# Attention's turn in another order: projection a turn later, values as 128x32 products, transposes together, modulations by DVE and POOL, banks in strict turn

## The chip, the cores and the metric

The kernel runs on one core of one Trainium2 chip. The metric is the device time of one execution, in microseconds (us). The kernel before takes 1629.52 us, the median of three runs (1629.29 to 1629.86).

## What is computed

The input x holds 128 sequences of 64 tokens with 128 channels, all in float32. Beside it come a condition vector for each sequence (cond) and a context of the same shape as x (ctx). Four layers follow one another:

```python
x = L0(x, cond, ctx)   # self-attention, cross-attention to ctx, MLP; modulation and gates from silu(cond)
x = L1(x, ctx, cond)   # cross-attention, both sides modulated
x = L2(x, cond, ctx)   # like L0, with the context normalised
x = L3(x, cond, ctx)   # attention of one head, router, three experts, gate
```

The attention of L0, L1 and L2 has 16 heads of 8 channels. For each of them: `xm = norm(x) * (1 + scale) + shift`, then q, k and v as products of xm (or of the context) with weights, `softmax(q k^T / sqrt(8)) v`, a projection, and a sum onto x (gated in self-attention). The change concerns these attentions alone: five of them, called here L0s, L0c, L1c, L2s and L2c (s: self, c: cross).

## The kernel before, in words

The 8192 tokens are 16 groups of 512 (8 sequences each); x stays in SBUF as 16 tiles. The program runs, one after another: L0s and L0c as one stream of 32 attention units (a unit is one group in one attention), the MLP of L0, then L1c, L2s and L2c as one stream of 48 units, the MLP of L2, and layer 3. The order of instructions is written out by hand (a manual schedule); each engine takes its own list strictly in order, and waits on semaphores where a tile isn't ready or a buffer isn't free.

In a unit:

- `prepare` (a generator: each `yield` ends a piece) loads the context (L394), measures x on DVE (`stats`, L313) and takes the power on POOL (L329, L330), normalises x on POOL (L369, L372), transposes on PE and takes the result out of PSUM (L342, then L347/L348, L359 or L379), makes k (`pk` L436, `kT` L438 on ACT, and on POOL the four masked copies `kbd` L444), q (`pq` L449, `qT` L451), and the values (`pvv` L459 on PE, two copies into `vbd` by ACT, L464 and L465).
- `scores` is called for two halves u = 0, 1: 16 products into `sc` (L478), which fills four PSUM banks and has one buffer; DVE takes the maximum `mx` (L485) and the difference `e` (L487).
- `turned` transposes a quarter of e into `pp` (L503; two banks, one buffer) and ACT takes the exponential `eT` (L507). It is called twice for each half, gg = 0 and 1.
- `weighted` multiplies by `vbd` into `po` (L520); ACT copies it to `o` (L528). The sums of the softmax come along as extra columns.
- `finish` sends the sums through DRAM (SP's queue: `sums`, `rc`, four shifts `o<-o`), takes the reciprocal on DVE (L547), sends it out (`recs`) and back spread over partitions (`rb`, L554), with two loads of the gate table (`gt`, L278) in self-attention; POOL then multiplies `oT = o * rb` (L557) and adds the bias onto x (L559); PE projects (`py`, L563); a cross unit adds py onto x on DVE (L565), a self unit makes `y = py * gate` on DVE (L568) and adds it onto x on POOL (L569).

`attend` weaves the units. Step k = 2i + u does the scores of unit i, half u, the first `turned` of the half before, the `weighted` of the half before that, then pieces of `prepare` and `finish` of neighbouring units (`go(prep, i + d)`, `go(fin, i - d)`), then the second `turned`, and more pieces. Two steps, one unit, make a turn.

The small PSUM tiles (`pk`, `pq`, `pvv`, `psT`, `po`, `py`) share one pool with two buffers, one tag "mm".

Of the kernel before, what the change touches and what calls it, by code (L numbers as in the profile page):

```python
# [59 lines left out]
def tile_kernel(ctx: ExitStack, tc: tile.TileContext, a: dict, out: bass.AP):  # L60
# [66 lines left out]
    class Places:  # L127
# [8 lines left out]

    pools = [
        Places(),
        stack.enter_context(tc.tile_pool(name="mm", bufs=2, space=PSUM)),
        None,  # L140
        None,
        None,
# [15 lines left out]
    def psum_for_mlp():  # L158
        take_psum(("ph", 4), ("py", 2))

    def mm(name):
        return pools[1].tile([P, 512], F32, tag="mm", name=name)

# [171 lines left out]

    def transposed(psum, src):

        ps = psum.tile([P, 512], F32, tag="mm", name="psT")  # L340
        for t in range(TT):
            T.transpose(ps[:, ts(t, P)], src[:, t, :], ident)  # L342
        return ps
# [23 lines left out]
    def normed_by_pool(pool, src, mv, rs, tag, engine=G):  # L367
# [6 lines left out]
            )  # L374
        return xn

    def copied(pool, ps, tag):
        t = pool.tile([P, NT], F32, tag=tag, name=tag)
        S.copy(t, ps)  # L379
        return t  # L380
# [5 lines left out]
    def prepare(pools, at):  # L386

        pool, psum = pools[:2]
        s, layer = at["s"], at["layer"]
        eps = 1e-5 if layer == "L1c" else 1e-6  # L390
        cross = layer[2] == "c"
        if cross:
            c = pool.tile([P, TT, P], F32, tag="c", name="c", bufs=3)
            nc.sync.dma_start(c, ctx_d[s])  # L394
        yield
        if layer == "L1c":
            mv = x_mv[:, s]
            rs = inv_std(pool, mv, eps)
        else:
            mv, rs = stats_of(pool, xs[s], eps)  # L400
        yield
        xn = normed_by_pool(pool, xs[s], mv, rs, "xn", V if at.get("first") else G)
        if cross:
            cn = c
            if layer != "L0c":
                cn = pool.tile([P, TT, P], F32, tag="cn", name="cn", bufs=1)
                for t in range(TT):
                    rs, nb = (v[:, s, ctx_eps.index(eps), t : t + 1] for v in (ctx_rs, ctx_nb))

                    if layer == "L1c" or s == 0:  # L410
                        G.tensor_scalar(cn[:, t, :], c[:, t, :], rs, nb, ALU.mult, ALU.add)
                    else:
                        S.activation(cn[:, t, :], c[:, t, :], AF.Identity, bias=nb, scale=rs)
        yield
        if layer == "L1c":
            kv_in = modulated_by_batch(pool, transposed(psum, cn), "L1_xcond_Wss_kv", 0, 1, s, "cm")
        elif cross:
            kv_in = copied(pool, transposed(psum, cn), "cm")
            if layer == "L0c":
                nc.sync.dma_start(ctxT[s], kv_in)  # L420
        else:
            q_in = kv_in = modulated_by_batch(
                pool, transposed(psum, xn), at["wmod"], 1, 0, s, by_dve=at.get("first", False)
            )
        yield
        if not cross:
            pass
        elif layer == "L1c":
            q_in = modulated(pool, transposed(psum, xn), "L1_xcond_Wss_q", 0, 1, s)
        else:  # L430
            q_in = copied(pool, transposed(psum, xn), "xm")
        yield


        pk = psum.tile([P, 512], F32, tag="mm", name="pk")
        T.matmul(pk, at["wk"], kv_in, start=True, stop=True)  # L436
        kT = pool.tile([P, NT], F32, tag="kT", name="kT")
        S.activation(kT, pk, AF.Identity, bias=at["bk"])  # L438
        i = turn[0] % 2
        turn[0] += 1  # L440
        vbd = vbds[i]
        kbd = pool.tile([P, 4, NB, L], F32, tag="kbd", name="kbd")
        for j in range(4):
            (V if at.get("first") else G).tensor_scalar(  # L444
                kbd[:, j], by_batch(kT), mask[:, j : j + 1], 1.0, ALU.mult, ALU.mult
            )
        yield
        pq = psum.tile([P, 512], F32, tag="mm", name="pq")
        T.matmul(pq, at["wq"], q_in, start=True, stop=True)  # L449
        qT = pool.tile([P, NT], F32, tag="qT", name="qT")  # L450
        S.activation(qT, pq, AF.Identity, bias=at["bq"])  # L451
        at.update(qT=qT, kbd=kbd)
        yield

        wv_pair = at["wv"].rearrange("p (i j d) -> p j i d", j=2, d=HD)
        pvv = psum.tile([P, NB, L], F32, tag="mm", name="pvv")
        for b in range(NB):
            for j in range(2):
                T.matmul(  # L459
                    pvv[ts(j, L), b, :], kv_in[:, ts(b, L)], wv_pair[:, j],  # L460
                    start=True, stop=True,
                )
        pv4 = pvv.rearrange("p b (i d) -> p b i d", d=HD)
        S.copy(vbd[0:L, :, :, 0:HD], pv4[0:L])  # L464
        S.copy(vbd[L:P, :, :, HD : 2 * HD], pv4[L:P])  # L465
        at["vbd"] = vbd
# [42 lines left out]
    def weighted(pools, at, u, eT):  # L509


        pool, psum = pools[:2]
        po = psum.tile([P, 2, 256], F32, tag="mm", name="po")
        e7 = eT.rearrange("p a h (g i t q) -> p a h g i t q", g=2, i=2, t=2)

        for i in range(2):
            for t2 in range(2):
                for h in range(2):
                    for g in range(4):
                        T.matmul(  # L520
                            po[ts(g, 32), i, ts(2 * t2 + h, L)],
                            at["vbd"][:, 4 * u + 2 * t2 + h, 2 * g + i, :],
                            e7[:, g // 2, h, g % 2, i, t2, :],
                            start=True, stop=True,
                        )
        if u == 0:
            at["o"] = pool.tile([P, 2, NT], F32, tag="o", name="o", bufs=3)
        S.copy(at["o"][:, :, ts(u, 256)], po)  # L528

    def finish(pools, at):  # L530
# [19 lines left out]

        if not cross:
            gt = gate_tile(pool, s, at["wp"])
        rb = pool.tile([P, NT], F32, tag="rb", name="rb", bufs=1)
        nc.sync.dma_start(rb, recs.unsqueeze(1).broadcast_to([16, HD, NT]))  # L554
        yield
        oT = pool.tile([P, NT], F32, tag="oT", name="oT", bufs=1)
        G.tensor_tensor(oT, o[:, 0, :], rb, ALU.mult)  # L557
        bias = proj_bias[at["wp"]].unsqueeze(1).broadcast_to([P, TT, P]) if cross else gt[:, :, 1, :]
        G.tensor_tensor(xs[s], xs[s], bias, ALU.add)  # L559
        yield  # L560
        py = psum.tile([P, TT, P], F32, tag="mm", name="py")
        for t in range(TT):
            T.matmul(py[:, t, :], oT[:, ts(t, P)], w[at["wp"]][:, 0], start=True, stop=True)  # L563
        if cross:
# [6 lines left out]
    def attend(pools, ats):  # L571
# [5 lines left out]
        def go(gens, i):  # L577
            if 0 <= i < n:
                next(gens[i], None)
# [8 lines left out]
        def step(k, between=(), late=()):  # L588
            i, u = divmod(k, 2)
            now, last, past = (  # L590
                halves[k - d] if 0 <= k - d < 2 * n else None for d in range(3)
            )
            if now:
                now["e"] = scores(pools, now["at"], now["u"])
            for f in between:
                f()
            if last:
                last["eT"] = pools[0].tile([P, 2, 2, 512], F32, tag="eT", name="eT")
                turned(pools, last["e"], last["eT"], 0)
            if past:  # L600
                weighted(pools, past["at"], past["u"], past["eT"])
            if u == 0:
                go(fin, i - 2)
                go(prep, i + 4)
                go(prep, i + 1)
                go(fin, i - 3)
            else:
                go(prep, i + 1)
            if last:
                turned(pools, last["e"], last["eT"], 1)  # L610
            if u == 0:
                go(prep, i + 2)
                go(prep, i + 3)
            else:
                go(prep, i + 1)
                go(prep, i + 2)
                for f in late:
                    f()
                go(fin, i - 1)
                go(fin, i - 2)  # L620
                go(prep, i + 4)

        return ahead, [lambda *more, k=k: step(k, *more) for k in range(2 * n + 5)]

    def attention_of(s, layer):
        if layer[2] == "s":
# [49 lines left out]
    def mlp(wmod, w1, b1, w2, b2, beside, mv_out=None, by_token=False):  # L676
# [50 lines left out]
            )  # L727

        def leave(d):
            pt = psum.tile([P, 512], F32, tag="mm", name="psB")  # L730
            for t in range(TT):
                T.transpose(pt[:, ts(t, P)], d["y"][:, ts(t, P)], ident)
            V.tensor_add(xs[d["s"]], xs[d["s"]], pt.rearrange("p (t c) -> p t c", t=TT))
# [456 lines left out]
    def stages():  # L1190
# [10 lines left out]
                later_tables[j]()  # L1201

        def beside_2(j):
            for f in l3_parts.get(j - 4, ()):
                f()

        heads_0, turns_0 = mlp(
# [4 lines left out]
            "L2_xcond_W_mod", "L2_xcond_W_mlp1", "L2_xcond_b_mlp1", "L2_xcond_W_mlp2",  # L1212
            "L2_xcond_b_mlp2", beside_2, by_token=True,
        )
        last = 5

        def into_mlp(steps, heads, turns):

# [15 lines left out]
        condition()  # L1234
        ahead_1(0, 0)
        first_mods[0]()
        ahead_1(0, 0, 1, 2, 0, 0, 1)
        psum_for_attention()

        steps_1[0]([lambda: ahead_1(2), lambda: clear(vbds[1]), lambda: ahead_1(1, 1, 0, 3)])  # L1240
        tables = first_tables()
        steps_1[1]()
        first_mods[1]()
# [10 lines left out]
        for s in range(2):  # L1254
            heads_0[3 + s] = lambda s=s, f=heads_0[3 + s]: (f(), load_context(s))
        rest = into_mlp(steps_1, heads_0, turns_0)
        second = [(0, 1, 2), (0,), (1, 0), (0, 0, 1, 2), (0, 1, 1, 2, 0, 0, 3, 3)]
        n_ = len(second)
        for f in rest[: -2 - n_]:
            f()  # L1260
# [64 lines left out]
```

## Time and profile before

| what | value |
|---|---|
| device time, median of 3 runs | 1629.52 us (1629.29 to 1629.86) |
| profiled execution: device time | 1626.31 us |
| profiled execution: span of its instructions | 1624.5 us |
| busy in 738 to 917 us (179 us, L2s): PE, DVE, ACT, POOL | 173.84, 162.28, 145.78, 140.45 us |
| busy in 930 to 1099 us (169 us, L2c): PE, DVE, ACT, POOL | 168.26, 151.57, 139.50, 119.84 us |
| mx L485, one | 2291 ns |
| e L487, one | 2291 ns |
| eT L507, one | 1030 ns |
| oT L557, one | 1276 ns |
| kbd L444, one of four | 690 ns |

The page gives for each engine the time in which it was busy, then groups of equal instructions with the mean duration of one, and the waits before them. The timeline lists instructions by start; the number after the start is the duration from the first start to the last end, and brackets tell how long the engine had been idle and what released it. A duration on DVE, ACT and POOL contains the fill of its pipeline: two that don't depend on each other start a little closer than the first one lasts. On PE the distance from start to start is what counts.

### The profile page before, as it was taken

How to read it: one execution, taken by the hardware profiler on the slowest of the kernel's cores; microseconds unless marked ns; L12 is line 12 of the kernel's file. 1: busy time of each engine (PE TensorE's matmuls, PEld its weight loads, DVE VectorE, ACT ScalarE, POOL GpSimd, SP SyncE). 2: the span in 40 equal slices, each digit the busy share in tenths (PEclk: the TensorE clock that was granted, in tenths of full speed). 3: DMA queues.
4: the chain of work that ended last, by engine and by line, in shares of the span. 5: the costliest groups of instructions: out<-in, count | busy, mean ns of one | idle time of the engine just before them, and what ended most of it. 6: DMA issues, size and time to landing. Idle time of an engine off the chain costs nothing.

```text
span 1624.5 us, 64028 instructions
## 1 busy us (share of the span) xinstructions
PE 1573.8 (97%) x27842; PEld 1086.8 (67%) x27842; DVE 1240.4 (76%) x1566; ACT 1035.5 (64%) x1710; POOL 1072.5 (66%) x1786
## 2 busy tenths in 40 slices
PE   6999999998999899999999999998999999999998
PEld 4676777776544577776777777776777566666665
DVE  7898998898555688899899889896443566666666
ACT  5788777776433678878888888886334544444443
POOL 6687787766888789887787876775875333333322
PEclk9999999999999999999999999999999999999999
DMA  8334453332111022211334432222533111111100
GB/s 209 85 82 99 107 127 92 83 83 72 55 36 55 16 63 61 72 44 50 90 82 102 104 88 73 62 56 59 130 81 76 31 39 37 40 33 36 34 12 19
DMA packets 146775, 112.65 MB, mean 69 GB/s; under 512 B 36357, under 2 KB 125247, under 8 KB 146495
## 3 DMA queue, kind: packets, MB, share of 16 engines
q1 hardware_dynamic: 146288, 108.53, 26.1%
q8 instruction: 219, 3.59, 0.9%
q14 instruction: 61, 0.50, 0.1%
q10 hardware_dynamic: 207, 0.03, 0.0%
HBM read 83.99 MB, written 14.02 MB: 60 GB/s over the span
## 4 chain that ended last, share of the span: by engine, by line
PE 83%; DVE 12%; ACT 3%; issue 1%; DMA 0%; SPq 0%; DVEq 0%
PE sc L478 10%; PE pp L503 9%; PE po L520 7%; PE ph L693 7%; PE ph L1080 6%; PE ph L1081 6%; DVE e L487 6%; DVE mx L485 6%; PE po L1111 5%; PE psT L342 5%; PE pk L436 5%; PE py L563 4%; PE py L709 4%; PE py L699 3%; PE pvv L459 3%; PE pq L449 3%
## 5 line engine op out<-in xcount | busy, mean ns | idle before, releaser
L507 ACT ACTIVATE eT<-pp 128x1024 f32<-128x1024 f32 x320 | 329.7, 1030 | 160.8 <-PE pp L503 160.7
L485 DVE TENSOR_REDUCE mx<-sc 128x32 f32<-128x2048 f32 x160 | 366.6, 2291 | 83.6 <-PE sc L478 83.6
L487 DVE TENSOR_TENSOR e<-sc,mx 128x2048 f32<-128x2048 f32 x160 | 366.6, 2291 | 5.4
L503 PEld LDWEIGHTS pp<-ident,e 64*128 64x128 f32 x5120 | 183.9, 138 | 140.1 <-ACT eT L507 44.7
L503 PE MATMUL pp<-ident,e 64*128 64x64 f32 x5120 | 227.7, 229 | 7.2 <-DVE e L487 4.7
L444 POOL TENSOR_SCALAR kbd<-kT,mask 128x512 f32<-128x512 f32 x316 | 212.4, 690 | 31.3 <-ACT kT L438 28.3
L372 POOL TENSOR_SCALAR xn<-x,nmu,rs 128x128 f32<-128x128 f32 x508 | 223.6, 453 | 13.3
L557 POOL TENSOR_TENSOR oT<-o,rb 128x512 f32<-128x512 f32 x80 | 102.1, 1276 | 163.5 <-DMA rb<-recs 62.9
L478 PE MATMUL sc<-kbd,qT 32*64 32x256 f32 x5120 | 179.2, 387 | 16.6 <-DVE e L487 15.6
L694 ACT ACTIVATE h<-ph,vec 128x512 f32<-128x512 f32 x128 | 87.3, 687 | 149.9 <-PE ph L693 149.7
L520 PE MATMUL po<-eT,vbd 128*32 128x64 f32 x10240 | 178.1, 221 | 1.4 <-issue 1.3
L1087 ACT ACTIVATE h<-h 128x512 f32<-128x512 f32 x112 | 70.6, 630 | 149.8 <-DVE h L1083 130.9
L520 PEld LDWEIGHTS po<-eT,vbd 128*32 128x32 f32 x10240 | 151.3, 110 | 14.4 <-issue 2.0
L330 POOL TENSOR_TENSOR rs<-rs,nhalf 128x4 f32<-128x4 f32 x128 | 130.2, 1017 | 10.7
L478 PEld LDWEIGHTS sc<-kbd,qT 32*64 32x64 f32 x5120 | 97.7, 131 | 53.0 <-issue 19.6
L1083 DVE TENSOR_TENSOR h<-ph,ab 128x512 f32<-128x512 f32 x112 | 76.9, 687 | 62.6 <-PE ph L1081 62.5
L1116 DVE SCALAR_TENSOR_TENSOR acc<-po,pr,acc 128x128 f32<-128x128 f32 x192 | 67.2, 350 | 44.1 <-PE po L1111 39.6
L1080 PE MATMUL ph<-nx,w 128*128 128x512 f32 x192 | 100.7, 607 | 0.0
L528 ACT COPY o<-po 128x512 f32<-128x512 f32 x160 | 95.7, 598 | 5.1 <-PE po L520 2.0
L1081 PE MATMUL ph<-u,w_ev 128*128 128x512 f32 x192 | 98.9, 597 | 0.0
L1111 PEld LDWEIGHTS po<-w_2o,h 128*128 128x128 f32 x768 | 92.1, 192 | 8.7 <-issue 8.4
L1104 POOL TENSOR_SCALAR g<-g 128x512 f32<-128x512 f32 x16 | 9.9, 622 | 132.1 <-ACT g L1103 132.1
(259 smaller groups left out, 2868.5 us busy)
## 6 DMA issues: line engine op xcount, KB each, us to landing
rb<-recs SPq DMA_DIRECT2D x80, 256.0 KB
c<-in_ctx_dram SPq DMA_DIRECT2D x64, 256.0 KB
o<-o SPq DMA_DIRECT2D x320, 32.0 KB
gt<-gate_L_xcond_sa_proj_w SPq DMA_DIRECT2D x32, 256.0 KB
gt<-gate_L_xcond_W_proj SPq DMA_DIRECT2D x32, 256.0 KB
gt<-gate_L_xcond_W_mlp SPq DMA_DIRECT2D x32, 256.0 KB
x<-in_x_dram SPq DMA_DIRECT2D x16, 256.0 KB
ctxT<-cm SPq DMA_DIRECT2D x16, 256.0 KB
```

The costliest lines, as they stand in the source:

```text
L330: G.tensor_tensor(rs, rs, nhalf, ALU.pow)
L372: engine.tensor_scalar(xn[:, t, :], src[:, t, :], nmu[:, t : t + 1], rs[:, t : t + 1], ALU.add, ALU.mult)
L444: (V if at.get("first") else G).tensor_scalar(kbd[:, j], by_batch(kT), mask[:, j : j + 1], 1.0, ALU.mult, ALU.mult)
L478: T.matmul(sc[ts(h, L), g, ts(t2, 256)], qT[ts(g, 32), ts(b, L)], kbd[ts(g, 32), :, b, :], start=True, stop=True,)
L485: V.tensor_reduce(mx, sc.rearrange("p g (m k) -> p (g m) k", k=L), AX.X, ALU.max)
L487: V.tensor_tensor(e, sc.rearrange("p g (m k) -> p (g m) k", k=L), mx.unsqueeze(2).broadcast_to([P, 32, L]), ALU.subtract,)
L503: T.transpose(pp[:, h, ts(4 * g2 + 2 * i + t2, L)], e6[ts(h, L), 2 * gg + g2, t2, i], ident[ts(h, L), ts(h, L)],)
L507: S.activation(eT[:, gg], pp, AF.Exp, scale=HD ** -0.5)
L520: T.matmul(po[ts(g, 32), i, ts(2 * t2 + h, L)], at["vbd"][:, 4 * u + 2 * t2 + h, 2 * g + i, :], e7[:, g // 2, h, g % 2, i, t2, :], start=T ...
L1080: T.matmul(ps, wn, d["nx"], start=True, stop=False)
L1081: T.matmul(ps, we, d["u"], start=False, stop=True)
L1111: T.matmul(po[:, ex, :], d[q][:, ts(t, P)], k3["w_2o"][:, q, :], start=r == 0, stop=r == 1)
```

## The change

The diff, cut to its core. `bank_tag` gives the small PSUM tiles two tags in strict turn (one buffer each); `normed_by_act` normalises x with ACT in the self units (all but the very first); the normalised context `cn` is made by ACT in L1c also (but for s = 0); the modulations of L1c (both sides) and of the self units go to DVE (multiply) and POOL (add) instead of eight ACT instructions; each transpose is a piece of its own, apart from the instruction that takes its result out of PSUM; values come as 64 products (two for each pair of sequence and half, 32 tokens each) with 32 columns of the array instead of 32 products with 64 columns (as the hardware counts them, two passes for each line of the program); `oT` is written over `rb`, which has two buffers; and `step` has the pieces in another order, with one step more in each stream.

```diff
     def mm(name):
-        return pools[1].tile([P, 512], F32, tag="mm", name=name)
+        return pools[1].tile([P, 512], F32, tag=bank_tag(), name=name)
...
+    def normed_by_act(pool, src, mv, rs, tag):
+        nb = pool.tile([P, TT], F32, tag="nmu" + tag, name="nb")
+        G.tensor_scalar(nb, means(mv), -1.0, 0.0, ALU.mult, ALU.add)
+        G.tensor_tensor(nb, nb, rs, ALU.mult)
+        xn = pool.tile([P, TT, P], F32, tag=tag, name=tag)
+        for t in range(TT):
+            S.activation(
+                xn[:, t, :], src[:, t, :], AF.Identity, bias=nb[:, t : t + 1],
+                scale=rs[:, t : t + 1],
+            )
+        return xn
...
-        xn = normed_by_pool(pool, xs[s], mv, rs, "xn", V if at.get("first") else G)
+        if cross or at.get("first"):
+            xn = normed_by_pool(pool, xs[s], mv, rs, "xn", V if at.get("first") else G)
+        else:
+            xn = normed_by_act(pool, xs[s], mv, rs, "xn")
...
-                    if layer == "L1c" or s == 0:
+                    if s == 0:
                         G.tensor_scalar(cn[:, t, :], c[:, t, :], rs, nb, ALU.mult, ALU.add)
                     else:
                         S.activation(cn[:, t, :], c[:, t, :], AF.Identity, bias=nb, scale=rs)
         yield
+        if cross:
+            ps = transposed(psum, cn)
+        yield
         if layer == "L1c":
-            kv_in = modulated_by_batch(pool, transposed(psum, cn), "L1_xcond_Wss_kv", 0, 1, s, "cm")
+            kv_in = modulated(pool, ps, "L1_xcond_Wss_kv", 0, 1, s, "cm")
         elif cross:
-            kv_in = copied(pool, transposed(psum, cn), "cm")
+            kv_in = copied(pool, ps, "cm")
...
+        yield
+        ps = transposed(psum, xn)
+        yield
+        if layer == "L1c":
+            q_in = modulated(pool, ps, "L1_xcond_Wss_q", 0, 1, s)
+        elif cross:
+            q_in = copied(pool, ps, "xm")
...
         else:
-            q_in = kv_in = modulated_by_batch(
-                pool, transposed(psum, xn), at["wmod"], 1, 0, s, by_dve=at.get("first", False)
-            )
+            q_in = kv_in = modulated(pool, ps, at["wmod"], 1, 0, s)
...
         for b in range(NB):
             for j in range(2):
-                T.matmul(
-                    pvv[ts(j, L), b, :], kv_in[:, ts(b, L)], wv_pair[:, j],
-                    start=True, stop=True,
-                )
+                for q in range(2):
+                    T.matmul(
+                        pvv[ts(2 * j + q, 32), b, :], kv_in[:, ts(2 * b + q, 32)], wv_pair[:, j],
+                        start=True, stop=True,
+                    )
...
-        oT = pool.tile([P, NT], F32, tag="oT", name="oT", bufs=1)
+        oT = rb
...
             if u == 0:
+                go(prep, i)
+                go(prep, i + 1)
+                go(prep, i + 2)
+            else:
                 go(fin, i - 2)
-                go(prep, i + 4)
                 go(prep, i + 1)
                 go(fin, i - 3)
-            else:
-                go(prep, i + 1)
+                go(prep, i + 2)
+                go(prep, i + 3)
             if last:
                 turned(pools, last["e"], last["eT"], 1)
+            go(prep, i + 2)
             if u == 0:
-                go(prep, i + 2)
+                go(fin, i - 2)
                 go(prep, i + 3)
+                go(prep, i + 4)
             else:
-                go(prep, i + 1)
-                go(prep, i + 2)
                 for f in late:
                     f()
                 go(fin, i - 1)
-                go(fin, i - 2)
-                go(prep, i + 4)
-
-        return ahead, [lambda *more, k=k: step(k, *more) for k in range(2 * n + 5)]
+
+        return ahead, [lambda *more, k=k: step(k, *more) for k in range(2 * n + 6)]
```

A self unit's turn then puts on each engine, between two scores: with u = 0 on PE `sc, pp, po, pvv, pk, pp` (a cross unit: `pk, psT, pp`); with u = 1 on PE `sc, pp, po, pq, py, psT, pp`, on ACT `eT, o, qT, xn, eT`, on DVE `mx, e, y, xm`, on POOL `oT, x, x, nb, nb, xm`. The two POOL adds onto x are those of the bias and of y. A cross unit has no second add onto x, and its xn is made on POOL after the bias.

The rest of the diff counts one step more at the joints with the MLPs, and hands out the first pieces of `prepare` in ten parts instead of eight.

## Prediction of the time

> **What bounds the kernel.** I read the page's busy times and its chain first, then the timeline of one turn in L2s and in L0c, then the busy times of a few narrow windows for the granted clock.
>
> ```profile
> PE 1573.8 (97%) x27842; PEld 1086.8 (67%) x27842; DVE 1240.4 (76%) x1566; ACT 1035.5 (64%) x1710; POOL 1072.5 (66%) x1786
> ...
> PE 83%; DVE 12%; ACT 3%; issue 1%; DMA 0%; SPq 0%; DVEq 0%
> ```
>
> PE carries the chain nearly everywhere. The timeline shows how close DVE follows (all engines, L2s, first column start, second duration):
>
> ```profile
> 813.46 2.29 DVE L487 TENSOR_TENSOR e<-sc,mx 128x2048 f32<-128x2048 f32 x1
> ...
> 815.36 1.02 ACT L507 ACTIVATE eT<-pp 128x1024 f32<-128x1024 f32 x1 [0.87 <-PE pp L503]
> 815.67 0.54 DVE L547 RECIPROCAL rc<-rc 128x64 f32<-128x64 f32 x1
> ...
> 815.84 1.12 PE L478 MATMUL sc<-kbd,qT 32*64 32x256 f32 x32
> 816.12 0.63 DVE L568 TENSOR_TENSOR y<-py,gt 128x512 f32<-128x512 f32 x1
> ...
> 816.89 0.71 PE L503 MATMUL pp<-ident,e 64*128 64x64 f32 x16
> 817.07 2.29 DVE L485 TENSOR_REDUCE mx<-sc 128x32 f32<-128x2048 f32 x1 [0.31 <-PE sc L478]
> 817.42 1.28 POOL L569 TENSOR_TENSOR x<-x,y 128x512 f32<-128x512 f32 x1
> 817.53 1.10 PE L520 MATMUL po<-eT,vbd 128*32 128x64 f32 x64
> ...
> 818.66 0.20 POOL L369 TENSOR_SCALAR nmu<-mv 128x4 f32<-128x4 f32 x1
> ...
> 819.39 2.29 DVE L487 TENSOR_TENSOR e<-sc,mx 128x2048 f32<-128x2048 f32 x1
> ```
>
> sc has one buffer, so scores and DVE take turns: sc to mx 1.23 us, mx to e 2.32, e itself 2.29, then the next sc: 5.92 for a half, 11.84 for a turn. PE's own list is hardly longer: turns start 11.91 us apart in L0s and L2s, 12.01 in L0c and L2c, 12.25 in L1c. So DVE caps the gain at 0.07, 0.17 and 0.41 us a turn: 32 x 0.07 + 32 x 0.17 + 16 x 0.41 = 14 us in all.
>
> **Part by part.** *Values as 128x32 products.* pvv takes 1.09 us from start to start (207.57 to 208.66 below). po has the same shape and number as the new form and takes 1.03 (816.89 + 0.64 = 817.53, the next at 1.03 where nothing is waited for). Worth 0.06 a turn at most; bounds nothing to 5 us over 80 units.
>
> *Fewer changes of shape on PE.* A transpose group ahead of another full-array product takes 0.44 us (MLP), ahead of sc 0.59; pq ahead of pp takes 1.06 and before its like 0.86. A cross turn has 13 such changes before and 10 after. The Trainium skill, TensorEngine Tiling (Array Packing), Key Properties, says that a change of tiling mode drains the array; it speaks for the change as these rows do.
>
> *What the order costs a cross turn.* Now the second pp stands right before sc. The next pp must wait until eT has read pp's only buffer: pp to eT 0.75, eT 1.03, release 0.05, so 1.83 against 0.64 + 1.05 = 1.69 on PE. And with banks in strict turn psT of the context takes pvv's bank, so it waits for both vbd copies:
>
> ```profile
> 207.57 1.15 PE L459 MATMUL pvv<-L_xcond_kv_w,cm 128*64 128x64 f32 x32
> ...
> 208.66 0.66 PE L342 MATMUL psT<-ident,xn 128*128 128x128 f32 x4
> 208.77 0.58 ACT L464 COPY vbd<-pvv 64x512 f32<-64x512 f32 x1
> ...
> 209.36 0.58 ACT L465 COPY vbd<-pvv 64x512 f32<-64x512 f32 x1
> ```
>
> The copies end 2.37 after pvv starts; on PE only pvv and pk (1.03 + 0.96) lie between. Half u = 0: pp 0.64, po 1.03, pvv to psT 2.4, psT 0.59, 1.83: 6.5. Half u = 1: 0.64, 1.03, pq to psT 1.9 (qT must leave the bank), 0.59, 1.83: 6.0. That is 12.5 instead of 12.0 in L0c; in L1c and L2c cn on ACT (4 x 0.385) ahead of eT adds 0.1. So +0.45 x 14, +0.57 x 14, +0.33 x 13 = +19 us (units without a successor to transpose left out). Other end, if none of these waits binds: DVE's 11.84, so -10 us. I take +19.
>
> *Modulations off ACT.* Eight ACT instructions (2.47 us) become one on DVE (0.69, L347) and one on POOL (1.04, L348). DVE has 1.5 us between e and mx in a half, and y with xm need 0.55 + 0.61: hidden. If that cover were gone it would cost 0.1 a turn.
>
> *xn on ACT in the self units: the expensive part.* With u = 1 ACT's list is eT, o, qT, xn, eT. xn needs nb from POOL; POOL's list is oT, x + bias, x + y, nb; and y stands on DVE behind this half's mx and e. Before, the same POOL add had only work behind it that nobody urgently awaited. Follow it from the start of sc (u = 1), all from rows above or named:
>
> - to y: 1.23 + 2.32 + 2.21 (815.67 - 813.46); y 0.63; DVE to POOL 0.08 (as at L348): 6.47.
> - x + y until the next POOL instruction 1.24 (818.66 - 817.42), two small nb 0.29 + 0.20, POOL to ACT 0.08 (an estimate, from the DVE to POOL wait): xn starts at 8.28.
> - xn 4 x 0.385 (as cn, L413), then eT 1.03 and 0.05: the next pp starts at 10.9, that is 4.95 after its sc instead of 1.05.
> - PE is in order, so po 0.64, pvv 1.03, pk 1.03, pp 1.06, 0.64 follow, and the next sc with u = 1 starts at **15.3**.
>
> A turn of 15.3 instead of 11.92 is +3.38. What waits behind the blocked xn: eT, so pp, so all of PE; DVE runs dry after e. The loop closes, nothing makes it up. It holds where unit i - 3 and unit i + 3 are both self: i = 3 to 12 in L0s and the same ten in L2s: 20 x 3.38 = **+68**. A second way round is as long. From sc (u = 0) the reciprocal starts at 5.76; oT follows 6.9 to 8.1 us later in self units, 7.6 in the middle (815.67 to 823.16 is 7.49; the recs, rb and gt transfers); oT, x, x and nb 4.28, xn 1.54, eT 1.08, PE's five 4.40: the next turn's sc (u = 1) starts at 17.05 + 7.6, and that is two turns less one plain half of 5.95: (23 + 7.6) / 2 = 15.3. Bounds: 0, if POOL came free early (its idle of 1.0 to 2.9 us ahead of oT is that same transfer, so it doesn't), to 20 x 4.1 = 82, if the transfer takes 9 us (9.5 is the longest that I find).
>
> *Seven more turns* (i = 2 of L0s; six around the joint of L1c and L2s) have only oT and the bias ahead of nb: the same way round without y's 1.24, and with 6 us for rb where no gt is loaded, gives (21.8 + 6) / 2 = 13.9, +2 to +3 each, **+16**.
>
> *Granted clock.* In such a turn PE idles about 3.7 us. The windows, each one 3.4 us long (columns: PE, PEld, DVE, ACT, POOL busy; clock; DMA):
>
> ```profile
> 1121.10:1124.50 3.40, 1.27 (x60) 1.23 (x64) 1.99 (x1) 1.32 (x2) 1.72 (x2) 0.99 0.19 58
> 1124.50:1127.90 3.40, 3.40 (x56) 3.01 (x46) 1.02 (x2) 1.15 (x2) 2.69 (x6) 0.50 0.17 37
> ...
> 400.80:404.20 3.40, 1.71 (x81) 1.59 (x81) 1.54 (x1) 1.32 (x2) 1.94 (x2) 1.00 0.14 34
> ```
>
> After a stretch with 1.27 us of PE work the clock was 0.50 for the next 3.4 us; after 1.71 us it was not. One row shows the price:
>
> ```profile
> 1125.25 2.08 PE L563 MATMUL py<-L_xcond_W_cproj,oT 128*128 128x128 f32 x8
> ```
>
> py lasts 2.08 instead of 1.08. An idle of 3.7 leaves at most about 1.55 us of work in one of the two stretches that it touches, nearer the first row. The half-speed 3.4 us fall on the PE list just released, where 1.7 us are lost if all lie behind the idle; if the stretch may begin anywhere from 1.9 us ahead of the idle's end to 1.5 us behind it, 0.8 to 1.7, on average 1.4: 20 x 1.4 = **+28**, and three of the seven +4. Bounds 0 to +40.
>
> The Trainium skill, TensorE: Matmul & The Clock Gate, in Part 1, has the clock fall to half after at least one idle window of about 3.4 us. The wait of 2.33 us in the row above already did it, so here the measurement decides. By the rule only some tenth of these idles would cover a whole window, and the sum would be about 29 us less.
>
> *At no cost:* oT in rb's place and two rb buffers (memory only); one step more at each joint, hidden under the MLP's PE work (up to 3 us if not); SP's queue keeps its order sums, recs, gt, rb, with rb's landing counted above.
>
> **Sum.** 68 + 16 + 28 + 4 + 19 = 135 us (pvv's 0.06 is inside the cross turns, where psT waits anyway; elsewhere it vanishes behind the waits). On the profiled execution's 1626.31 that is 1761; the median of the runs stands 3.2 higher, so 1764.
>
> **Rivals.**
> 1. *The same chain, the clock stays full.* 1629.5 + 68 + 16 + 19 = 1732. For it: 2.3 and 2.9 us of idle (at 400 and 546 us) left the clock alone. Against: those fell on two stretches, with 1.7 us of work in each. Chance 0.20.
> 2. *The POOL chain doesn't bind, the bank and eT waits do:* 1629.5 + 19 = 1648. That needs nb ahead of y's add on POOL, which the lists contradict. Chance 0.10.
> 3. *Faster: DVE's loop becomes the only bound.* Place: sc's single buffer. If xn on ACT is released before qT ends (4.6 us into the half) and psT is not held by vbd, each turn falls to 11.84: -14, so 1615. It decides from the point where nb is ready 3.7 us earlier than I work out. For it: ACT sheds 1.4 us in the self turns, and pq's wait for xm (0.17 to 0.34 us in L2s and L1c) goes. Chance 0.04; no change between, 0.02.
> 4. The forecast, 0.64.
>
> **How the numbers follow.** The predicted 1764 is the forecast's; its own range is 1740 to 1800 (82 instead of 68, 40 instead of 28, and clock in all seven). The 8-in-10 range reaches to rival 1 with its cross turns at their other end: 1629.5 + 68 + 16 - 10 = 1703; 1700 to 1805. Left out: rivals 2 and 3 and little else. Slower by over 0.2% (what a measurement of this kernel can tell from no change) 0.94, same 0.02, faster 0.04.
>
> **What would show it.** Right: in L2s sc starts 5.9 and some 10.8 us apart by turns; xn on ACT waits for POOL nb; pp waits for eT about 4 us; the clock in L0s and L2s is well under 1. L0c turns of 12.5 and psT released by vbd. Wrong: xn starts right after qT, or sc stays 5.9 apart throughout.

## The result, and the profile after

The changed kernel takes 1810.66 us (median of four runs, 1805.23 to 1812.0) against 1629.4 us for the kernel before (four runs, 1627.48 to 1629.86). The ratio is 1.1109, 95% interval 1.1084 to 1.1133: **11% slower**. The forecast was 1764 with a range to 1805, so the direction and most of the size were there, and 47 us were missing. The profiled execution took 1811.44 us, its span is 1809.5 us.

The page of the kernel after: busy times, the granted clock in 40 slices, the chain that ended last, and two of the costliest groups (at the end of a group's line stands the engine's idle time just ahead of it and what ended most of it).

```profile
PE 1619.6 (90%) x30402; PEld 1127.0 (62%) x30402; DVE 1270.0 (70%) x1613; ACT 1007.3 (56%) x1518; POOL 1045.9 (58%) x1680
...
PEclk9898899999999999998889899999999999999999
...
PE 63%; ACT 18%; POOL 11%; issue 4%; DVE 3%; DMA 1%; SPq 0%; POOLq 0%; ACTq 0%; DVEq 0%
...
L526 PE MATMUL pp<-ident,e 64*128 64x64 f32 x5120 | 234.3, 233 | 118.8 <-ACT eT L530 109.0
...
L389 ACT ACTIVATE xn<-x,nb,rs 128x128 f32<-128x128 f32 x124 | 50.9, 482 | 100.2 <-POOL nb L386 100.2
```

PE no longer carries the chain alone: ACT and POOL hold 29% of it, "issue" 4%, and the clock was cut in the slices of L0s and L2s. xn waited 100 us for nb, and pp 109 us for eT; that pp would wait for eT behind xn was forecast.

The stages, worked out from the starts of the sc groups in the timeline of both kernels:

| stage | before, us | after, us | difference |
|---|---|---|---|
| L0s | 193.5 | 260.4 | +66.9 |
| L0c | 187.3 | 208.0 | +20.8 |
| MLP between | 146.3 | 145.2 | -1.1 |
| L1c | 195.1 | 212.9 | +17.8 |
| L2s | 192.2 | 264.1 | +72.0 |
| L2c | 187.2 | 198.0 | +10.8 |
| MLP and layer 3 | 507.3 | 505.3 | -2.0 |

One turn of L2s after (timeline, all engines; start, duration, engine, line; in brackets the idle time and who ended it):

```profile
930.55 1.94 PE L543 MATMUL po<-eT,vbd 128*32 128x64 f32 x64
...
932.26 1.75 PE L482 MATMUL pvv<-L_xcond_W_qkv,xm 128*32 128x64 f32 x64
...
933.95 1.13 PE L459 MATMUL pk<-xm,L_xcond_W_qkv 128*128 128x512 f32 x2
934.09 0.58 ACT L487 COPY vbd<-pvv 64x512 f32<-64x512 f32 x1 [0.95 <-PE pvv L482]
934.68 0.58 ACT L488 COPY vbd<-pvv 64x512 f32<-64x512 f32 x1
...
935.29 0.69 ACT L461 ACTIVATE kT<-pk,vec 128x512 f32<-128x512 f32 x1
...
936.08 2.70 POOL L464 TENSOR_SCALAR kbd<-kT,mask 128x512 f32<-128x512 f32 x4 [7.91 <-ACT kT L461]
...
939.14 1.02 POOL L336 TENSOR_TENSOR rs<-rs,nhalf 128x4 f32<-128x4 f32 x1
...
940.13 1.28 POOL L580 TENSOR_TENSOR rb<-o,rb 128x512 f32<-128x512 f32 x1
...
941.37 1.28 POOL L582 TENSOR_TENSOR x<-x,gt 128x512 f32<-128x512 f32 x1
941.41 0.68 DVE L591 TENSOR_TENSOR y<-py,gt 128x512 f32<-128x512 f32 x1
941.75 1.12 PE L501 MATMUL sc<-kbd,qT 32*64 32x256 f32 x32
...
942.60 1.26 POOL L592 TENSOR_TENSOR x<-x,y 128x512 f32<-128x512 f32 x1
...
944.11 0.20 POOL L386 TENSOR_TENSOR nb<-nb,rs 128x4 f32<-128x4 f32 x1
...
944.35 1.65 ACT L389 ACTIVATE xn<-x,nb,rs 128x128 f32<-128x128 f32 x4 [3.88 <-POOL nb L386]
...
945.90 1.00 ACT L530 ACTIVATE eT<-pp 128x1024 f32<-128x1024 f32 x1
...
946.96 0.86 PE L526 MATMUL pp<-ident,e 64*128 64x64 f32 x16 [4.09 <-ACT eT L530]
```

sc starts at 941.75 and the next pp only at 946.96, 5.21 us later (forecast 4.95). But look at who was late. y was done at 942.09 and POOL took it up at 942.60, since POOL was still busy; and POOL was late because it had stood idle for 7.91 us until ACT delivered kT at 936. kT in turn was held on ACT's list by the two vbd copies (the second ends at 935.26, pk at 935.08). So the ring is pp, po, pvv, the vbd copies, kT, then kbd, rs, oT (written as rb), x + bias, x + y and nb on POOL, then xn, eT and pp again. The forecast had y, or the transfer of rb, as its last link. In each of the 20 turns in which POOL adds both the bias and y ahead of nb, it took up y's add 0.5 us after y was done and never stood idle between kbd and nb, and oT did not wait for rb.

The clock beside it, in windows that are the clock's own stretches (columns: PE, PEld, DVE, ACT, POOL busy; clock; DMA):

```profile
926.87:930.28 3.41, 0.47 (x14) 0.47 (x16) 3.38 (x2) 2.55 (x5) 1.21 (x3) 1.00 0.13 29
930.28:933.69 3.41, 3.41 (x128) 3.29 (x128) 1.25 (x4) 1.61 (x2) 0.00 (x0) 0.50 0.29 87
933.69:937.10 3.41, 3.23 (x74) 1.79 (x68) 0.22 (x1) 2.76 (x4) 1.02 (x2) 1.00 0.76 166
```

PE worked 0.47 us in one stretch, and the next stretch ran at half clock, over po and pvv. A stretch at half clock stands in every full self turn.

The second cost is in the cross turns. L0c, PE alone:

```profile
292.68 0.51 PE L482 MATMUL pvv<-L_xcond_kv_w,cm 128*32 128x64 f32 x21
...
295.08 0.86 PE L482 MATMUL pvv<-L_xcond_kv_w,cm 128*32 128x64 f32 x43 [1.90 <-issue]
...
297.20 0.66 PE L348 MATMUL psT<-ident,c 128*128 128x128 f32 x4 [0.20 <-ACT vbd L488]
```

The last line is the bank wait that was forecast. The one above it is new: PE stops inside pvv, after 21 of its 64 products, and nothing that the profile shows is waited for. Over the span the kernel after has these (PE's waits: total, times, longest), where the kernel before has only three stops of 1.3 us together in po:

```profile
PE pvv L482 <- issue: 17.4, 23, 2.1
...
PE po L543 <- issue: 6.0, 9, 1.4
```

### The profile page after: what moved, and what is told of

It is laid out like the page before. It is cut to its first block, busy times and chain, and to the rows that moved or that the text cites. A ratio compares the mean times of both kernels' runs of the same rounds, so it can differ in the third digit from the quotient of the medians.

```text
span 1809.5 us, 68772 instructions
## 1 busy us (share of the span) xinstructions
PE 1619.6 (90%) x30402; PEld 1127.0 (62%) x30402; DVE 1270.0 (70%) x1613; ACT 1007.3 (56%) x1518; POOL 1045.9 (58%) x1680
## 4 chain that ended last, share of the span: by engine, by line
PE 63%; ACT 18%; POOL 11%; issue 4%; DVE 3%; DMA 1%; SPq 0%; POOLq 0%; ACTq 0%; DVEq 0%
PE po L543 8%; PE pp L526 8%; ACT eT L530 6%; PE ph L717 6%; PE ph L1104 5%; PE ph L1105 5%; PE pvv L482 5%; PE po L1135 5%; POOL kbd L464 4%; PE psT L348 3%; PE py L733 3%; PE py L723 3%; PE pq L469 3%; ACT xn L389 3%; ACT vbd L488 2%
## 5 line engine op out<-in xcount | busy, mean ns | idle before, releaser
L464 POOL TENSOR_SCALAR kbd<-kT,mask 128x512 f32<-128x512 f32 x316 | 212.7, 690 | 284.3 <-ACT kT L461 284.0
L526 PE MATMUL pp<-ident,e 64*128 64x64 f32 x5120 | 234.3, 233 | 118.8 <-ACT eT L530 109.0
L526 PEld LDWEIGHTS pp<-ident,e 64*128 64x128 f32 x5120 | 189.2, 142 | 236.0 <-ACT eT L530 187.2
L543 PE MATMUL po<-eT,vbd 128*32 128x64 f32 x10240 | 201.9, 237 | 6.1 <-issue 6.0
L543 PEld LDWEIGHTS po<-eT,vbd 128*32 128x32 f32 x10240 | 172.2, 120 | 20.6 <-issue 7.0
L580 POOL TENSOR_TENSOR rb<-o,rb 128x512 f32<-128x512 f32 x80 | 101.9, 1274 | 138.2 <-DMA rb<-recs 79.2
L378 POOL TENSOR_SCALAR xn<-x,nmu,rs 128x128 f32<-128x128 f32 x384 | 169.8, 455 | 10.3
L389 ACT ACTIVATE xn<-x,nb,rs 128x128 f32<-128x128 f32 x124 | 50.9, 482 | 100.2 <-POOL nb L386 100.2
```

The source lines that it names most:

```text
L378: engine.tensor_scalar(xn[:, t, :], src[:, t, :], nmu[:, t : t + 1], rs[:, t : t + 1], ALU.add, ALU.mult)
L464: (V if at.get("first") else G).tensor_scalar(kbd[:, j], by_batch(kT), mask[:, j : j + 1], 1.0, ALU.mult, ALU.mult)
L526: T.transpose(pp[:, h, ts(4 * g2 + 2 * i + t2, L)], e6[ts(h, L), 2 * gg + g2, t2, i], ident[ts(h, L), ts(h, L)],)
L543: T.matmul(po[ts(g, 32), i, ts(2 * t2 + h, L)], at["vbd"][:, 4 * u + 2 * t2 + h, 2 * g + i, :], e7[:, g // 2, h, g % 2, i, t2, :], start=T ...
```

## The experiments

Experiments 1 to 7 are one run each, 8 to 12 medians of 4 to 12 runs; the kernel before took 1626 to 1629 us beside them. A turn is measured from one sc with u = 0 to the next. The theory was that the +181 us come from xn on ACT behind POOL's list, from the half clock that this brings, and from instructions that reach PE late; the rivals stand with each experiment.

### 1. xn of the self units on POOL again

```diff
-        if cross or at.get("first"):
+        if True:
             xn = normed_by_pool(pool, xs[s], mv, rs, "xn", V if at.get("first") else G)
```

> The changed kernel with xn of the self units made on POOL again (all else as changed). Theory (eT waits behind xn on ACT, xn waits for nb at the end of POOL's list): turns of L0s and L2s fall from 17.1 us to about 12.0, the clock there returns to 1.00, ACT waits for nb no more; the whole about 1670 us. Rival (the new order on PE and the banks cost the time, xn on ACT only fills a gap): turns stay above 16 us, the whole above 1780 us.

Measured: 1737.78 us, 73 us less than the kernel after; neither theory's number. L0s lasts 233.0 us instead of 260.4. The waits of pp for eT are gone, but PE's list of waits begins with a new one:

```profile
PE pk L459 <- POOL xm L354: 57.5, 26, 4.9
PE pvv L482 <- issue: 22.9, 29, 1.9
```

The modulation's add (xm) now stands on POOL behind oT, x, x and xn, and oT waits for rb. Turns alternate between 12.3 and about 17 us. Taking xn off ACT gives back 73 us, and the same lateness of POOL has a second way to PE, through the modulation, which the prediction had costed at nothing.

### 2. xn on ACT, but nb made with the statistics

```diff
             mv, rs = stats_of(pool, xs[s], eps)
+        if not (cross or at.get("first")):
+            nb = negated(pool, mv, rs, "xn")
         yield
```

(`negated` holds the two instructions on POOL that made nb in `normed_by_act`.)

> xn stays on ACT, but POOL makes nb in the piece with the statistics, ahead of oT, the bias and y's add. Theory (what stands ahead of nb on POOL is the cost): the way round pp, po, pvv, pk, kT, kbd, rs, nb, xn, eT is about 11.8 us, so turns of 12 to 12.5 in L0s and L2s, the whole 1670 to 1690 us. Rival (ACT's own 1.65 us of xn ahead of eT is the cost): turns stay above 15 us, the whole above 1770 us.

Measured: 1709.8 us, 101 us less than the kernel after, though 20 us above the theory's range. xn on ACT no longer waits behind the list, and self turns alternate between 11.9 and 13.4 to 15.7 us. What is left is again pk behind POOL's xm (33.4 us, 16 times, longest 5.8). It isn't ACT that makes xn dear, but nb at the end of POOL's list.

### 3. Values as 32 products of 64 columns

```diff
-                for q in range(2):
-                    T.matmul(
-                        pvv[ts(2 * j + q, 32), b, :], kv_in[:, ts(2 * b + q, 32)], wv_pair[:, j],
...
+                T.matmul(
+                    pvv[ts(j, L), b, :], kv_in[:, ts(b, L)], wv_pair[:, j],
...
```

> The changed kernel with pvv as 32 products with 64 columns again. Theory (PE stops in the middle of po and pvv because its instructions come too late; 256 of them now stand side by side in 2 us): those stops of 0.3 to 2.3 us go, u = 0 halves of the cross units all at 6.3 to 6.4 us, the whole about 27 us less, 1783 us. Rival (the stops belong to the place, next to po, and not to the number of instructions): within 6 us of 1810. The self turns stay at 17.1 in both.

Measured: 1802.62 us, 8 us less; that is one run, and the kernel after itself spreads over 7 us. The stops named issue fall from 25.8 us (pvv, po, sc and pk together) to 6.3, and L0c's turns become an even 12.6 us (198.5 us instead of 208.0). But 12.6 is more than the best turns after, 12.40; and the self turns stay at 17.1 to 17.3, since there PE has idle time to be late in. The stops went as the theory had it; the time fell by a third of what it had.

### 4. Work for PE in its idle time

Four products of 128x512 into po's bank, overwritten by po, ahead of the first pp of the 20 full self turns:

```diff
+            if past and u == 0 and past["at"]["layer"][2] == "s" and 3 <= past["at"]["s"] <= 12:
+                po = pools[1].tile([P, 2, 256], F32, tag=bank_tag(), name="po")
+                flat = po.rearrange("p a b -> p (a b)")
+                for _ in range(4):
+                    T.matmul(
+                        flat, past["at"]["wq"], past["at"]["qT"], start=True, stop=True
+                    )
...
-                weighted(pools, past["at"], past["u"], past["eT"])
+                weighted(pools, past["at"], past["u"], past["eT"], po)
```

> Four extra 128x512 products (3.4 us of PE work whose result is overwritten) ahead of the first pp in the u = 0 half of 20 self turns, where PE idles 4.1 us; nothing else changes. Theory (the half clock costs 1.4 to 1.7 us in each of these turns): the clock stays at 1.00 there, turns fall from 17.1 to about 15.4, the whole about 34 us less, 1776 us. Rival (the waits on POOL and ACT set the turn, half clock hides under them): within 6 us of 1810, or more if the added work is in the way.

Measured: 1781.7 us: **29 us less by giving PE 74 us more work** (20 times 3.70). The mean clock rises from 0.968 to 0.987, turns in L2s are mostly 15.0 to 15.8. The theory held. PE's timeline:

```profile
894.67 3.70 PE L626 MATMUL po<-qT,L_xcond_W_qkv 128*128 128x512 f32 x8
898.79 0.71 PE L526 MATMUL pp<-ident,e 64*128 64x64 f32 x16 [0.42 <-ACT eT L530]
899.43 1.10 PE L544 MATMUL po<-eT,vbd 128*32 128x64 f32 x64
900.35 1.08 PE L482 MATMUL pvv<-L_xcond_W_qkv,xm 128*32 128x64 f32 x64
```

pp still waits for eT, but po and pvv take 1.1 us each instead of 1.94 and 1.75: the half clock costs about 1.45 us a turn (29 us over 20 turns). The warm turn is 15.8 us on average over the 20, where 15.3 was forecast.

### 5. The projection behind xn on POOL's list

```diff
                 go(prep, i + 1)
-                go(fin, i - 3)
                 go(prep, i + 2)
                 go(prep, i + 3)
+                go(fin, i - 3)
```

> The changed kernel with the projection piece (py, y and POOL's add of y) behind the piece that makes nb and xn, so nb no longer stands behind y's add. Theory A (the prediction's: the way round closes through DVE's y): self turns are left with the other way round, 13.9 us plus some 1 us of half clock, about 15, the whole 40 us less, 1770 us. Theory B (it closes through kT and the four kbd on POOL; y is there in time): only the 1.24 us of one POOL add leave the way round, turns of 15.5 to 16.5, or 17.07 still where the half clock holds it, the whole 0 to 25 us less, 1785 to 1810 us.

Measured: 1783.24 us; self turns alternate between 14.3 and 16.7, 15.5 on average. The time lies between the two theories. But the move brought a wait of its own, py for ACT's qT (23.8 us, 70 times, none after), which lengthens the other half from 6.1 to 6.5 or 6.6 us, so the turns can't tell the theories apart. POOL's wait for kT at kbd stays its longest (242.7 us, against 284.0 after). Inconclusive; that kT and kbd close the ring rests on the timeline above.

### 6. Experiment 1, the self modulation on ACT, values of 64 columns

> xn on POOL, the self units' modulation back on ACT (eight instructions) and pvv with 64 columns; order of the pieces, banks, transposes and L1c as changed. Theory (with xn on POOL alone what was left was pk waiting up to 4.2 us for the modulation's add, which POOL reaches only after rb's transfer; and PE's late instructions): no wait of pk on POOL, L0s and L2s at 11.9 to 12.2 us a turn, cross turns at 12.6, the whole 1650 to 1658 us. Rival (rb's transfer holds the self turns in another way too, through py or oT): turns above 12.8 us, the whole above 1668 us.

Measured: 1677.8 us, the rival's side, with turns just under its 12.8. The long waits and the half clock are gone from the self turns, 60 us less than in 1, but they are 12.7 us long: now pvv waits for ACT's eight modulations (15.7 us, 25 times). The cross turns stay at 12.5 to 12.6.

### 7. Experiment 6, transposes again behind the second pp

```diff
                 go(prep, i + 1)
-                go(prep, i + 2)
             else:
...
-                go(prep, i + 2)
                 go(prep, i + 3)
             if last:
                 turned(pools, last["e"], last["eT"], 1)
             go(prep, i + 2)
+            go(prep, i + 2)
```

> Like the run before it, but each transpose behind the second pp of the half again instead of ahead of it. Theory (pp right ahead of sc makes the next pp wait for eT, 1.83 against 1.69 us, and psT right behind pk waits for the vbd copies): cross turns fall from 12.6 to about 12.0, self turns stay at 11.9, the whole about 25 us less than the run before, 1625 to 1633 us. Rival (the banks in strict turn or the projection's new place hold the cross turns): cross turns stay above 12.4 us.

Measured: 1657.6 us, 20 us less than experiment 6. Undisturbed turns of all kinds fall to 12.1, so the transposes' place, with the bank waits, is worth 20 us in sum, although the stops named issue in po and pvv grow from 5.0 to 16.8 us. But 1625 to 1633 was expected. Of the 31 us to the kernel before, PE's waits show where 17 lie:

```profile
PE po L542 <- issue: 12.8, 12, 2.2
...
PE pvv L481 <- issue: 4.0, 6, 1.1
```

Stops, although the number of PE's instructions is that of the kernel before.

### 8. The kernel before, with its values as 64 products of 32 columns

The value change alone.

> The kernel before with nothing changed but pvv as 64 products with 32 columns. Theory (the stops need 256 PE instructions of po and pvv side by side; here pp stands between them): no stop within pvv, cross turns from 12.01 to about 11.95, the whole 0 to 4 us less, 1625 to 1629 us. Rival (the longer program itself brings PE's instructions too late): stops of 0.3 us and more within pvv or po in many turns, the whole 5 to 25 us more.

Measured: 1651.93 us, ratio 1.0148 (1.0122 to 1.0173). **The rival was right: the narrower products cost 24 us by themselves** (by the ratio). Where nothing stops, the halves with pvv fall from 6.09 to 6.04 us, the gain that the prediction counted. But the stops, which stand now mostly in po, whose code is unchanged, cost more: the 29 halves that hold one are 24.0 us longer in sum than the same halves before, all other halves 4.6. Among PE's waits:

```profile
PE po L521 <- issue: 13.7, 22, 1.7
...
PE sc L479 <- issue: 2.7, 4, 1.4
```

What they wait for can be counted. The table of DMA queues has a queue "instruction" (packets, MB, share), first before, then after:

```profile
q8 instruction: 219, 3.59, 0.9%
```

```profile
q8 instruction: 239, 3.92, 1.0%
```

239 packets times 256 is 61,184, and the trace of after holds 61,204 instructions of PE (60,804 products and weight loads, and 400 that wait or drain); before, 219 times 256 is 56,064 for 56,128. So a packet of 16,384 bytes holds 256 PE instructions. Counting PE's instructions from the start, I looked where the stops inside a group stand (those of over 0.22 us, pp left out; the last two columns are over the attention stages):

| kernel | stops | place: 256 x (packets landed) and | from landing to going on, us | time from one such place to the next, median | packet landed ahead of its place, median |
|---|---|---|---|---|---|
| before | 3 | 193 | 1.4 to 1.6 | 5.15 | 3.16 |
| after | 33 | 193 | 1.2 to 1.6 | 5.35 | 2.77 |
| experiment 7 | 18 | 193 | 1.3 to 1.6 | 5.25 | 3.13 |
| experiment 8 | 27 | 193 | 1.2 to 1.7 | 4.69 | 2.39 |

All 81 stand at the same place of a packet, and PE goes on 1.2 to 1.7 us after a packet landed. These are waits for the next 256 instructions. A packet starts some 0.7 to 1.1 us (median) after PE passed the place before, takes 1.1 us, and at least 1.2 us more pass before it is used: that is some 3 us, and 5 us or more when it starts late, against 5 us of work. With 32 columns the same work holds more instructions, so the next place comes sooner (4.69 us instead of 5.15).

### 9 and 10. The kernel before, with modulations by DVE and POOL

In 9 only those of L1c's context:

```diff
-            kv_in = modulated_by_batch(pool, transposed(psum, cn), "L1_xcond_Wss_kv", 0, 1, s, "cm")
+            kv_in = modulated(pool, transposed(psum, cn), "L1_xcond_Wss_kv", 0, 1, s, "cm")
```

In 10 also those of the self units (`modulated` in place of `modulated_by_batch`, but for the first).

> The kernel before, with one edit: in L1c the context's modulation is one multiply on DVE and one add on POOL instead of eight ACT instructions. In the kernel before, the half u = 1 of an L1c turn lasts 6.33 us because pq waits for ACT's cm and eT stands behind cm. Theory (DVE and POOL have room for it, ACT was late): these halves fall to about 6.05, 13 turns by 0.3 = -4 us, so 1625 (1623 to 1627). Rival (POOL, busy 11.4 of 12.25 us in such a turn, becomes late with 1.04 us more): cm or xm late by POOL, time 1631 or more.

> The last kernel, and the self units' modulation by DVE and POOL as well, with the transposes where the kernel before has them. Theory (the add on POOL is in time, since here oT and the bias stand behind it or well ahead): self halves with the modulation fall from 5.99 to 5.92, another 2 us less, so 1623 (1620 to 1626). Rival (the add stands on POOL behind oT, which waits for the transfer of rb, and pk waits for it, as in the kernel after with xn on POOL): 2 to 4 us more in many self turns, 1640 or more, with waits of pk for POOL's xm.

Measured for 9: 1626.31 us, ratio 0.9996 (0.9986 to 1.0006): no difference. L1c's halves with pq fall to 6.09, as the theory says, but the other half rises to 6.27, since py now waits for POOL's oT; turns are 12.4 in the later half of L1c. Gain and loss cancel.

Measured for 10: 1636.93 us, ratio 1.0059 (1.0043 to 1.0074): 0.6% slower, and neither theory had the reason. pk waits for POOL once only (4.8 us, in the first turn of L0s). Self turns are 12.1 instead of 11.9 because of DVE:

```profile
895.99 2.29 DVE L489 TENSOR_TENSOR e<-sc,mx 128x2048 f32<-128x2048 f32 x1
898.20 0.54 DVE L549 RECIPROCAL rc<-rc 128x64 f32<-128x64 f32 x1
898.66 0.63 DVE L570 TENSOR_TENSOR y<-py,gt 128x512 f32<-128x512 f32 x1
899.21 0.68 DVE L347 TENSOR_TENSOR xm<-psT,mod_L_xcond_W_mod 128x512 f32<-128x512 f32 x1
899.80 2.28 DVE L487 TENSOR_REDUCE mx<-sc 128x32 f32<-128x2048 f32 x1
```

No gap is left. mx starts 1.42 us after its sc (898.38) instead of 1.23, and the half lasts 6.17 instead of 5.99. The prediction had counted 1.5 us of room and 0.55 + 0.61 for y and xm; in this order the reciprocal's 0.46 stands there too.

### 11. The kernel before, with its banks in strict turn

The two tags of the change alone.

> The kernel before, with one edit: the small PSUM tiles have two tags with one buffer each, in strict turn, instead of one tag with two buffers. Theory (two buffers of one tag were handed out in turn anyway): within 1.5 us of the kernel before. Rival (strict turn makes psT or po wait for an earlier reader, as the prediction had it for the cross turns): 0.3 us or more in most turns, 1640 or more, with new waits of PE for ACT's vbd or o.

Measured: 1631.49 us, ratio 1.0030 (1.0018 to 1.0042), between the two. The attention stages don't change (the five sum to 955.9 us, and 955.3 before); the 4 us lie in the MLP between L0c and L1c (150.4 instead of 146.3), where two stretches of 3.4 us run at half clock (none before) and pq waits once 2.0 us for ACT's cm. (The idle of 2.33 us ahead of the first of these stretches is in the kernel before too, at full clock.) In the order of before, the tags alone bring no bank wait into the turns; those of the cross turns need the new order of the pieces.

### 12. The kernel before, with pvv right behind po

```diff
-        pq = ...
-        qT = ...
-        yield
-
         wv_pair = at["wv"].rearrange("p (i j d) -> p j i d", j=2, d=HD)
...
         at["vbd"] = vbd
+        pq = ...
+        qT = ...
+        yield
```

> The kernel before, with the values' products (32, 64 columns, as they were) placed right behind po and ahead of pq; the number of instructions is unchanged. po and pvv then give PE 96 products (192 instructions with their weight loads) in 2.1 us without a long product between. Theory (PE's instructions come late where the dense groups stand together, whatever their total): stops named issue in po and pvv of 10 us or more in sum over the span, time 1645 or more. Rival (only the greater number of instructions makes them late): such stops stay under 3 us as in the kernel before, and the time rises only by what pp in front of sc costs, about 0.14 us a turn where no transpose stands between, 80 turns at most, so 1628 to 1640.

Measured: 1645.26 us, ratio 1.0102 (1.0072 to 1.0131). The time fits the theory, the reason doesn't: stops in po and pvv sum to 4.1 us, not 10. The self turns of 12.2 and L1c's of 12.6 come from plain waits instead, pq for ACT's o 0.24 us in each, and pp right ahead of sc, where 25 waits of 0.18 us bear the name issue too, but at no fixed place of a packet. So dense groups side by side don't explain the stops of experiment 7.

No kernel here beats the kernel before; 9 equals it.

## Why the prediction was wrong

The forecast's terms against the differences of the two traces (185 us between the profiled executions, 181 between the medians):

| term | forecast, us | measured, us |
|---|---|---|
| 20 full self turns, with the clock | 68 + 28 | 106 |
| other turns of L0s, L2s and the joint with L1c, with the clock | 16 + 4 | 42 |
| cross turns | 19 | 41 |
| MLPs and layer 3 | 0 | -3 |

What failed are two terms of the sum, the other turns and the cross turns with the price of the values; and one link of the chain was named wrongly.

**xn on ACT, 20 turns:** the end of the chain (nb late on POOL's list, then xn, eT and pp) was right, and so nearly was the size. pp 5.2 us after sc (4.95), halves of 11.0 and 6.1 (10.8 and 5.9), a warm turn of 15.8 (15.3), clock 1.45 a turn (1.4). The named last link was wrong: not y and not rb, but kT and kbd on POOL. The prediction's list for POOL began with oT and left out kbd and rs, which stand ahead of it. That the numbers lie close together all the same is luck.

**Other turns: a step that failed.** "Only oT and the bias ahead of nb: the same way round without y's 1.24" gave +2 to +3 for each of seven turns. From the second of them on, POOL is late because of kbd (idle 7.8 to 9.0 us ahead of it), so leaving out y frees little: the last two turns of L1c and the first three of L2s take 16.9, 15.8, 16.8, 17.0 and 15.5 us instead of 12, that is 22 us for five, and the half clock came there too, after idles of 2.8 to 3.9 us. The turn i = 2 of L0s, the seventh, did not grow (11.9). The other 20 us were not in the sum at all: the first two turns of L0s (5 us), and the last three of L0s and of L2s (15 us). Into these last the lateness runs on, since a wait for xn falls in the first half of the next turn.

**Cross turns:** the base was right, 6.34 + 6.06 = 12.40 where nothing else happens (forecast 12.5), with psT released by vbd and pp by eT. The rest was missed: 44 of these turns (all but the last of L0c and of L2c and the last two of L1c) lie 29 us above that, and the stops named issue in them sum to 20 us.

**Values: a step that failed.** "Bounds nothing to 5 us" looked at the duration of the products only. Experiment 8 has the price in the order of before, 24 us. In the order after, taking the narrower products back gave 8 us (experiment 3, one run): the stops fell by 19.5 us, but the undisturbed half u = 0 of L0c grew from 6.34 to 6.51 us. The trace of before could have warned: three of its stops in po bear the name issue, and the table of queues has 3.59 MB of instructions.

**Modulations at no cost:** true in the order after only as long as xn is later still. Once it isn't, pk waits 57 us for POOL's add (experiment 1). In the order before they cost 0.2 us a self turn (experiment 10); "0.1 a turn if that cover were gone" was half of it.

**Clock:** The rows of the trace were the right guide. The wait of 2.33 us that the prediction names is this one of the kernel before:

```profile
1123.23 0.71 PE L503 MATMUL pp<-ident,e 64*128 64x64 f32 x16 [2.33 <-DVE e L487]
```

The two idles that left the clock alone, at 400 and 546 us, had 2.60 and 1.71, and 1.85 and 1.74 us of PE work in their stretches, not 1.7 in each. The Trainium skill, TensorE: Matmul & The Clock Gate, Part 1, has the gate watch a free-running window of about 3.4 us; the stretches agree, with 3.41 us each. By its rule the clock falls after an idle window; here 0.47 us of work in a window did not save it, and the measurement decides.

**Rivals:** the clock did not stay full (1), the chain bound (2), and DVE's loop of 11.84 us did not become the bound of any stage (3; for it stood that ACT sheds 1.4 us in the self turns, but its own rows give 2.47 - 1.54 = 0.9).

**Open:** why experiment 7, with the instruction count and much of the order of before, has 17 us of stops and before 1.3. Its packets start up to 5.4 us after the place before (before 3.3). Packets start later where more other data begins to move in the 3 us behind that place (before: 0.59 us on average with under 60 KB, 1.45 us with over 500 KB), but in the four kernels of the table the correlation is only 0.25 to 0.44. What decides isn't shown.

## What to carry to other kernels

When a step is moved onto an engine that takes its list in order, follow the list *backwards* until you find the instruction that really waits, here kbd for kT, and not the last one that you added; otherwise a changed neighbourhood (the joints) is mis-sized. Price products by their number as well as their duration: in the kernel before, where PE is 97% busy, 64 small ones for 32 larger ones (over 80 units) cost 24 us although the group takes no longer. And where PE must idle for some microseconds, work without use can be cheaper than idling, as in experiment 4.

## What the runs showed of the hardware

- In L0s after, the half-clock stretches come at 83.78, 100.84, 117.91, 134.97 us and so on, 17.07 apart, which is five stretches of 3.413. The turns there last 17.10 to 17.15 us, so a stretch falls into each of them; whether one pulls the other isn't shown.
- In the traces of before and after, half clock followed stretches at full clock with up to 1.56 us of PE work, and none with 1.72 us or more; one with 1.51 us was spared.
- PE's instructions arrive 256 at a time, in packets of 16,384 bytes that take 1.1 us and are used 1.2 to 1.7 us after they land; where 256 instructions are worked off too soon after the last packet, PE stops for 0.2 to 2.3 us in the middle of a group, with no wait named.
